# Order of loads, stores and norms in the head stage of a graph kernel

## The chip, the cores and the metric

The kernel runs on one core of one Trainium2 chip. The metric is the device time of one execution in microseconds (us); the median of several runs stands for a kernel. Besides, one execution is taken with the hardware profiler, and every view below is of that one.

## The reference

The input is x, 128 graphs of 128 nodes with 256 features, and an adjacency matrix for each graph. Layer 0 normalises x over the features, takes the positive part h, and computes from h a convolution branch (a 1x1 convolution, batch norm, relu, a convolution with 17 taps along the nodes, batch norm, relu with h added), a message branch and a gated recurrent cell. Layer 1 is a set of small graph convolutions on the first 25 nodes. All is in float32. The part that matters here is the beginning of layer 0:

```python
h = jnp.maximum(_layernorm(x, axis=-1), 0.0)
...
xc = jnp.transpose(x, (0, 2, 1))
h = _bn(_conv1d(xc, conv1_w, 0), bn1_g, bn1_b, bn1_m, bn1_v)
h = jax.nn.relu(h)
h = _bn(_conv1d(h, conv2_w, 8), bn2_g, bn2_b, bn2_m, bn2_v)
```

(the x inside the branch is the h of the first line).

## The kernel before, in words

The graphs are worked on in 32 blocks of four. The 17-tap convolution is done in the frequency domain: the nodes of a graph are transformed to 68 frequencies, multiplied there by the transformed taps, and transformed back. The kernel has three stages: the heads (from 0 to about 286 us), the spectral products (to about 466 us) and the gates with layer 1 (the rest).

The change lies in the heads. There the order of the instructions of every engine is the order in which the program writes them down (a manual schedule); each engine, and each queue that issues DMAs, works through its own list in that order and waits where an operand isn't ready. For each block the heads do the following.

- `head_load` (L198) brings the block's x to a tile `ln` of 0.5 MB. There are four such tiles (`ahead = 4`), so the load for block i+4 can start once the transposes of block i have read theirs. SP issues it.
- `head_stats` (L208, L209, L212 on DVE, L214 on GpSimd) gives mean and reciprocal deviation. It comes in two parts of two graphs each.
- `head_norm` (L221 and L227 on DVE, L224 on ACT) normalises: ACT does two graphs of the block, DVE the other two.
- `head_turn` transposes the block on PE (L237), ACT takes the positive part into a tile `ht` (L238), and SP stores it to DRAM (`htd`, L239) for the third stage. "Turn" in the text is this step.
- `head_conv1` multiplies by the 1x1 weights, in two halves (L251 on PE), and DVE's maximum with a row stands for batch norm's shift and relu (L254).
- `head_sums` makes even and odd parts on GpSimd (L262 to L264).
- `head_spectra` transforms the block before (L280 on PE; ACT L291 and DVE L289 copy to X).

Beside this run the spectra of the taps, 16 units in all. A unit has three steps, each a batch of small matmuls (L180) whose results ACT (L189) and in part DVE (L187) copy to a tile `sp` of 2.2 MB, of which there are two. After its last step the unit is stored to DRAM (`vd`, L191); the spectral stage reads it back as `v` (L344). `some_spectra`, called `between` in the loop, does one step. The loop calls it twice in odd iterations (in the middle and at the end) and once in even ones (at the end), so that a unit takes two iterations; when a unit is found finished at the end of an odd iteration, its store is issued, the taps of a later unit are loaded (L166), and the next unit's first step is done in the same call.

Iteration i of the loop in `heads` works on several blocks at once: it turns block i+1, does conv1 for block i, takes statistics of block i+3, normalises block i+2 and transforms block i-1. So even blocks are turned in odd iterations. Its order before the change is: load of block i+4; statistics part 0; conv1 half 0; (odd: tap step); sums; norms; conv1 half 1; statistics part 1; turn and store of h; sums; tap step; spectra.

The PSUM banks of this stage are given out in a fixed rotation of eight: conv1 takes one for each half, a turn two, a tap step four, the spectra four. A matmul therefore waits until the engine that empties the bank given out eight before has done so.

Of the kernel before, what the change touches and what calls it, by code (L numbers as in the profile page):

```python
# [17 lines left out]
BB = 4  # L18
# [57 lines left out]
def gnn_kernel(ctx: ExitStack, tc: tile.TileContext, io, out0: bass.AP, out1: bass.AP):  # L76
# [94 lines left out]
    def weight_spectra(pool, c, q, w2):  # L171

        sp = pool.tile([P, LW, WCH], F32, tag="sp", name="sp", bufs=2)
        n = WCH // 4
        for s0 in range(0, n, STEP):
            s1 = min(s0 + STEP, n)
            ps = [bank() for _ in range(4)]
            for j in range(s1 - s0):
                for r in range(4):
                    nc.tensor.matmul(ps[r][:, j * LW:(j + 1) * LW], w2[32 * r:32 * r + KW, s0 + j, :],  # L180
                                     gt[32 * r:32 * r + KW, :], start=True, stop=True)
            for r in range(4):
                o0 = r * n + s0
                dst = sp[:, :, o0:o0 + s1 - s0]
                s = ps[r][:, :(s1 - s0) * LW].rearrange("p (j d) -> p d j", d=LW)
                if r == 3 and s1 < n:
                    nc.vector.tensor_copy(dst, s)  # L187
                else:
                    nc.scalar.copy(dst, s)  # L189
            yield  # L190
        nc.sync.dma_start(vd[c, q], sp)  # L191


    xs, stats, hcs, h1s, evens = ({} for _ in range(5))
# [1 line left out]
    def head_load(pool, ahead, i, queue):  # L196
        xs[i] = pool.tile([P, BB, D], F32, tag="ln", name="ln", bufs=ahead)
        queue.dma_start(xs[i], x[i])  # L198
# [28 lines left out]
            nc.vector.tensor_scalar(xs[i][:, b, :], xs[i][:, b, :], mv[:, b, 0:1], rs[:, b:b + 1],  # L227
                                    op0=ALU.subtract, op1=ALU.mult)

    def head_turn(wk, i):  # L230

        ln = xs.pop(i)
        ht = wk.tile([P, C, T], F32, tag="ht", name="ht", bufs=2)
        for c in range(C):
            ps = bank()
            for b in range(BB):
                nc.tensor.transpose(ps[:, b * N:(b + 1) * N], ln[:, b, c * P:(c + 1) * P], ident)  # L237
            nc.scalar.activation(ht[:, c, :], ps, AF.Relu)  # L238
        nc.sync.dma_start(htd[i], ht)  # L239
        hcs[i] = ht  # L240

# [52 lines left out]
    def heads(wk, xk, ep, ahead, X, between, consts):  # L294

        for i in range(NBLK + 1):
            more = i < NBLK
            if i + ahead < NBLK:
                head_load(xk, ahead, i + ahead, nc.sync)
            if i == 0:  # L300
                head_conv1(wk, 0, 0)
                between()
                head_sums(ep, 0, 0)
                head_norm(1, wk)
                head_conv1(wk, 0, 1)
                head_turn(wk, 1)
                head_sums(ep, 0, 1)
                head_stats(wk, 2)
                between()
                head_norm(2, wk)  # L310
                head_stats(wk, 3)
                continue
            if i + 3 < NBLK:
                head_stats(wk, i + 3, (0,))
            if more:
                head_conv1(wk, i, 0)
            if i % 2:
                between()
            if more:
                head_sums(ep, i, 0)  # L320
            if i + 2 < NBLK:
                head_norm(i + 2, wk, BB // 2)
            if more:
                head_conv1(wk, i, 1)
            if i + 3 < NBLK:
                head_stats(wk, i + 3, (1,))
            if i + 1 < NBLK:
                head_turn(wk, i + 1)
            if more:
                head_sums(ep, i, 1)  # L330
            between()
            head_spectra(X, i - 1)
            if i == 2:
                next(consts)
# [72 lines left out]
    with front as es:  # L407
        hk = es.enter_context(tc.tile_pool(name="hk", bufs=1))
        xp = es.enter_context(tc.tile_pool(name="xp", bufs=1))
        X1 = xp.tile([P, C, NP_ - NB, 2, P], F32)  # L410
        order = es.enter_context(ExitStack())
        order.enter_context(tc.manual_schedule(engines={nc.gpsimd.engine}))
        early = es.enter_context(ExitStack())
        xe = early.enter_context(tc.tile_pool(name="xe", bufs=1, side="right"))
        X0 = xe.tile([P, C, NB, 2, P], F32)
        X = X0, X1
        with ExitStack() as ws:

            ws.enter_context(tc.manual_schedule())

            xk = ws.enter_context(tc.tile_pool(name="xk", bufs=1, side="right"))
            wp = ws.enter_context(tc.tile_pool(name="wp", bufs=1))
            ahead = 4
            todo = [(c, q) for c in range(C) for q in range(D // WCH)]
            nc.scalar.dma_start(gt, io["gt"])
            nc.scalar.dma_start(vec, io["vec"])

            taps = [taps_load(wp, *todo[0], nc.sync, split=4, amid=[lambda: head_load(xk, ahead, 0, nc.sync)])]
            spectra = []
            ones = X1[:, 0, 0].rearrange("p k g -> p (k g)")  # L430
            nc.vector.memset(ones, 1.0)

            def rouse(n):
                ps = bank()
                for _ in range(n):
                    nc.tensor.matmul(ps[:, :2 * P], ones[:, :P], ones, start=True, stop=True)

            def some_spectra(k=1):
                for _ in range(k):
                    if not spectra and todo:  # L440
                        spectra.append(weight_spectra(wp, *todo.pop(0), taps.pop(0)))
                    if spectra and next(spectra[0], STOP) is STOP:
                        spectra.pop(0)
                        if len(todo) > 1:
                            taps.append(taps_load(wp, *todo[1], nc.sync))
                        some_spectra()

            constant_loads()
            head_load(xk, ahead, 1, nc.sync)
            taps.append(taps_load(wp, *todo[1], nc.sync))  # L450
            for k in range(2, ahead):
                head_load(xk, ahead, k, nc.sync)
            nc.sync.dma_start(fw, row("fw", 5))
            consts = constants(wp)
            head_stats(hk, 0)
            rouse(3)
            some_spectra()
            rouse(4)
            next(consts)
            some_spectra()  # L460
            next(consts)
            head_norm(0)
            next(consts)
            rouse(2)
            head_turn(hk, 0)
            head_stats(hk, 1)
            some_spectra()
            heads(hk, xk, wp, ahead, X, some_spectra, consts)
            while spectra or todo:
                some_spectra()  # L470
        turns.close()
        banks[:] = [ctx.enter_context(tc.tile_pool(name="psum", bufs=8, space=bass.MemoryType.PSUM, reuse_waits="tile")), None]

        bp = es.enter_context(tc.tile_pool(name="bp", bufs=1, reuse_waits="tile"))
        spectral(bp, (X0, 0), 0, NB, {})
        early.close()
        gw = ctx.enter_context(tc.tile_pool(name="gw", bufs=1, side="right", reuse_waits="tile"))
        idm = gw.tile([P, N], F32)
        wms = gw.tile([P, C, 2, MW], F32)
        bms = gw.tile([P, 2, MW], F32)  # L480
        swm = gw.tile([P, 3, MW], F32)
        wih = gw.tile([P, 2 * C, 3 * D], F32)
        whh = gw.tile([P, C, 3 * D], F32)
        sw = [gw.tile([P, 3, 3, P], F32, name=f"sw{k}") for k in range(3)]

        def gate_load(to, what):
            tc.keep_in_program_order(nc.sync.dma_start(to, what))

        def gate_loads():
            gate_load(wms, io["wms"].rearrange("(c p) (q o) -> p c q o", p=P, q=2))  # L490
            yield
            gate_load(idm, io["idm"])
            gate_load(bms.rearrange("p q o -> p (q o)"), row("bms", 2 * MW))
            for name, w in (("whh", whh), ("wih", wih)):
                for c in range(w.shape[1]):
                    yield
                    gate_load(w[:, c], io[name][c * P:(c + 1) * P])

        loads, sums = gate_loads(), gate_weights()

        def gate_steps(p):
            next(loads, None)
            if p in (36, 40, 44, 52, 56, 60, 64):
                next(sums, None)

        amid = {p: lambda p=p: gate_steps(p) for p in range(NB, NP_, 4)}
        spectral(bp, (X1, NB), NB, NP_, amid)
        for _ in sums:
            pass
        order.close()  # L510
# [799 lines left out]
```

## Time and profile before

| | us |
|---|---|
| runs, median of 3 | 1870.97 |
| runs, lowest to highest | 1866.61 to 1873.89 |
| the profiled execution | 1868.6 |
| its span, first to last instruction | 1866.8 |
| PE busy in the span | 1824.8 (98%) |
| DVE busy | 1359.8 (73%) |
| GpSimd busy | 790.4 (42%) |
| ACT busy | 732.3 (39%) |

A busy PE isn't PE at its peak, since matmuls are pipelined and their ends are modelled. What decides is the chain of work that ended last: it follows the last instruction back, at each step to what released it. Over the whole span 82% of it is PE, 9% DMA (7% loads of x) and 4% DVE. In windows of 20 us the heads show PE at 16.6 to 20 us busy, DVE at 12 to 18, ACT at 9 to 16, DMA at shares of 0.66 to 0.87, and a granted PE clock between 0.83 and 1.0 of full speed; the spectral stage after 300 us shows PE at 20 of 20 and the clock at 1.0.

In the views, PE is the matmuls and PEld their weight loads, POOL is GpSimd, SPq is SP's queue of DMA issues, and L251 is line 251 of the kernel. "<-" names what ended a wait.

### The profile page before, as it was taken

Reading aid. Unit: us, or ns where it says so; the run is one execution under the profiler, and the core shown is the slowest. Engines: PE = TensorE matmul, PEld = TensorE weight load, DVE = VectorE, ACT = ScalarE, POOL = GpSimd, SP = SyncE. Lnnn points to the kernel's source line nnn. Section 1 sums busy time; section 2 is a strip of 40 time slices with the busy share of each in tenths; the row PEclk is TensorE's granted clock in tenths of the full one; section 3 lists DMA queues with packets and bytes.
Section 4 is the critical chain, followed back from the end, with each engine's and each line's share of the span. In section 5 each row is a group of like instructions: output and inputs, shape, how many; then the busy total and the mean of one; then the engine's idle time right before and its main releaser. Section 6 shows DMA issues by size and latency. Waiting matters only on the chain.

```text
span 1866.8 us, 34711 instructions
## 1 busy us (share of the span) xinstructions
PE 1824.8 (98%) x12552; PEld 1581.5 (85%) x12552; DVE 1359.8 (73%) x3331; ACT 732.3 (39%) x1624; POOL 790.4 (42%) x993
## 2 busy tenths in 40 slices
PE   8898999999999999999999999999999999999998
PEld 6777787888888888888788888888788888888787
DVE  6776766777887888788656678887756678787553
ACT  5555551111434333343344443343343443333334
POOL 4665665577344354354312235444412243544100
PEclk9899999999999999999999999999999999999999
DMA  7777769998733333334324433334333433332134
GB/s 286 274 282 282 277 272 305 337 334 268 229 90 77 86 83 84 76 85 113 83 82 109 128 94 75 74 79 117 73 82 94 120 106 86 82 72 79 24 95 135
DMA packets 279870, 267.47 MB, mean 143 GB/s; under 512 B 170870, under 2 KB 247371, under 8 KB 277651
## 3 DMA queue, kind: packets, MB, share of 16 engines
q1 hardware_dynamic: 274515, 247.32, 45.8%
q10 hardware_dynamic: 5184, 17.93, 2.4%
q8 instruction: 100, 1.64, 0.4%
q14 instruction: 71, 0.58, 0.1%
HBM read 168.84 MB, written 96.35 MB: 142 GB/s over the span
## 4 chain that ended last, share of the span: by engine, by line
PE 82%; DMA 9%; DVE 4%; POOL 1%; SPq 1%; issue 1%; ACT 0%; DVEq 0%; ACTq 0%; POOLq 0%
PE bank L714 43%; DMA ln<-in_x_dram 7%; PE bank L371 6%; PE bank L1041 5%; PE bank L982 5%; PE bank L615 5%; PE bank L366 3%; PE bank L665 3%; PE bank L594 3%; PE bank L251 3%; PE bank L280 1%; PE bank L961 1%; PE bank L891 1%; DMA nt<-in_adjN_dram 1%; PE bank L571 1%
## 5 line engine op out<-in xcount | busy, mean ns | idle before, releaser
L714 PE MATMUL bank<-t,sw 128*128 128x256 f32 x1152 | 291.9, 380 | 0.8 <-POOL t L689 0.4
L727 POOL TENSOR_TENSOR u<-u,m 128x256 f32<-128x256 f32 x128 | 94.9, 741 | 463.8 <-ACT m L725 409.0
L714 PEld LDWEIGHTS bank<-t,sw 128*128 128x128 f32 x1152 | 215.0, 191 | 33.4 <-issue 2.8
L714 PE MATMUL bank<-t,wih 128*128 128x256 f32 x768 | 200.3, 384 | 0.0
L714 PEld LDWEIGHTS bank<-t,wih 128*128 128x128 f32 x768 | 143.5, 190 | 29.0 <-DVE o L754 6.6
L251 PE MATMUL bank<-wc,ht 128*128 128x256 f32 x512 | 134.9, 416 | 0.0
L363 POOL TENSOR_TENSOR vs<-v 128x256 f32<-128x256 f32 x134 | 101.0, 779 | 57.0 <-DMA v<-vd 30.5
L251 PEld LDWEIGHTS bank<-wc,ht 128*128 128x128 f32 x512 | 101.8, 207 | 18.7
L714 PE MATMUL bank<-xc,wih 128*128 128x256 f32 x384 | 114.9, 381 | 0.9 <-ACT xc L598 0.8
L714 PE MATMUL bank<-t,whh 128*128 128x256 f32 x384 | 114.7, 380 | 0.1
L714 PE MATMUL bank<-xn,wih 128*128 128x256 f32 x384 | 114.3, 379 | 0.0
L1041 PE MATMUL bank<-w,hh 128*125 128x256 f32 (+9 forms) x480 | 113.6, 380 | 0.1
L714 PE MATMUL bank<-ht,whh 128*128 128x256 f32 x384 | 110.3, 381 | 0.3 <-DVE m L625 0.3
L638 ACT ACTIVATE msg<-msg 128x512 f32<-128x512 f32 x64 | 36.8, 622 | 182.0 <-DVE msg L634 182.0
L598 ACT ACTIVATE xc<-xc,bn 128x512 f32<-128x512 f32 x64 | 46.2, 722 | 150.4 <-DVE xc L597 150.4
L1041 PEld LDWEIGHTS bank<-w,hh 128*125 128x125 f32 (+9 forms) x480 | 84.6, 178 | 18.0 <-DVE hh L987 1.2
L982 PE MATMUL bank<-ax,w 128*128 128x500 f32 (+9 forms) x352 | 94.5, 404 | 1.0 <-DVE xc L597 1.0
L732 DVE TENSOR_TENSOR u<-bank,u 128x256 f32<-128x256 f32 x128 | 53.5, 418 | 50.2 <-PE bank L714 49.6
L208 DVE BATCH_NORM_STATS2 st<-ln 128x6 f32<-128x256 f32 x128 | 51.8, 405 | 51.1 <-DMA ln<-in_x_dram 51.1
L368 ACT COPY k<-bank 128x256 f32<-128x256 f32 x67 | 25.0, 372 | 145.8 <-PE bank L366 68.7
L714 PEld LDWEIGHTS bank<-xn,wih 128*128 128x128 f32 x384 | 73.1, 190 | 9.8
L714 PEld LDWEIGHTS bank<-xc,wih 128*128 128x128 f32 x384 | 72.2, 191 | 10.5 <-ACT xc L598 1.4
(224 smaller groups left out, 4582.5 us busy)
## 6 DMA issues: line engine op xcount, KB each, us to landing
vd<-sp SPq DMA_DIRECT2D x16, 2176.0 KB
v<-vd SPq DMA_DIRECT2D x34, 1024.0 KB
w<-in_w_dram SPq DMA_DIRECT2D x40, 512.0 KB
ln<-in_x_dram SPq DMA_DIRECT2D x32, 512.0 KB
htd<-ht SPq DMA_DIRECT2D x32, 512.0 KB
yd<-ys ACTq DMA_DIRECT2D x32, 512.0 KB
ht<-htd SPq DMA_DIRECT2D x64, 256.0 KB
ym<-yd SPq DMA_DIRECT2D x32, 512.0 KB
```

The source lines that it names most:

```text
L251: nc.tensor.matmul(pv[:, s, :], ht[:, c, (2 * h + s) * N:(2 * h + s + 1) * N], wc1[:, c, :], start=c == 0, stop=c == C - 1)
L363: nc.gpsimd.tensor_tensor(vs[:, c], vi[c], vr[c], op=ALU.subtract)
L366: nc.tensor.matmul(p1[:, :D], a[:, c], vs[:, c], start=c == 0, stop=c == C - 1)
L371: nc.tensor.matmul(ps[:, k * D:(k + 1) * D], u[:, c], w[c], start=c == 0, stop=c == C - 1)
L594: nc.tensor.matmul(ps[:, b * N:(b + 1) * N], ym[:, 2 * h + b, o * P:(o + 1) * P], idm, start=False, stop=b == 1)
L615: nc.tensor.matmul(ps[:, b, :], d[:, b * N:(b + 1) * N], w, start=True, stop=True)
L665: nc.tensor.matmul(ps[:, b * N:(b + 1) * N], msg[:, b, c * P:(c + 1) * P], e[:, b, :], start=True, stop=True)
L714: nc.tensor.matmul(ps, w, d, start=n == 0, stop=n == len(pairs) - 1)
L727: nc.gpsimd.tensor_tensor(got["u4"], got["u2"], got["m5"], op=ALU.add)
L732: nc.vector.tensor_tensor(got["u3"], ps, got["u2"], op=ALU.add)
L982: nc.tensor.matmul(pv[:, q - q0, :], w1s[k5 + g][:, c, q * P:(q + 1) * P], xv[:, c], start=c == 0, stop=c == C - 1)
L1041: nc.tensor.matmul(ps[:n1, :D], hh[:, q, at:at + n1], w2s[k5 + g][:, q, :], start=q == 0, stop=q == HID // P - 1)
```

## The change

Four things are altered, all in the heads.

1. The load of x for block i+5 is issued in iteration i, inside the turn, between ACT's relu and the store of h. Before, the load of that block was issued at the start of iteration i+1. (The first turn, before the loop, issues the load of block 4.)
2. In iterations from 1 on, the norms of block i+2 come first, ahead of conv1's first half and its maximum; the first part of the statistics of block i+3 comes after the sums, where the norms were.
3. A finished unit of tap spectra isn't stored at once. Two halves of it, each 68 of the 136 columns, are put on a list, and each later tap step first issues one half from that list.
4. The loop after the heads runs until that list is empty, too.

```diff
-        nc.sync.dma_start(vd[c, q], sp)
+        for d in range(0, LW, LW // 2):
+            stores.append((vd[c, q, :, d:d + LW // 2], sp[:, d:d + LW // 2]))
...
-    def head_turn(wk, i):
+    def head_turn(wk, i, reload=None):
...
             nc.scalar.activation(ht[:, c, :], ps, AF.Relu)
+        if reload:
+            reload()
         nc.sync.dma_start(htd[i], ht)
...
-            if i + ahead < NBLK:
-                head_load(xk, ahead, i + ahead, nc.sync)
+            reload = None
+            if i + 1 + ahead < NBLK:
+                reload = lambda i=i: head_load(xk, ahead, i + 1 + ahead, nc.sync)
...
-            if i + 3 < NBLK:
-                head_stats(wk, i + 3, (0,))
+            if i + 2 < NBLK:
+                head_norm(i + 2, wk, BB // 2)
             if more:
                 head_conv1(wk, i, 0)
             if i % 2:
                 between()
             if more:
                 head_sums(ep, i, 0)
-            if i + 2 < NBLK:
-                head_norm(i + 2, wk, BB // 2)
+            if i + 3 < NBLK:
+                head_stats(wk, i + 3, (0,))
...
             if i + 1 < NBLK:
-                head_turn(wk, i + 1)
+                head_turn(wk, i + 1, reload)
...
+            def some_spectra():
+                if stores:
+                    nc.sync.dma_start(*stores.pop(0))
+                advance()
...
-            head_turn(hk, 0)
+            head_turn(hk, 0, lambda: head_load(xk, ahead, ahead, nc.sync))
...
-            while spectra or todo:
+            while spectra or todo or stores:
                 some_spectra()
```

`advance` is the old body of `some_spectra`.

## The prediction

> **What bounds the kernel now.** Read first: the chain of work that ended last, in order of time, for the first 300 us. From about 33 to 240 us it consists of two kinds of link, PE's matmuls and loads of x (the columns are start, length, what ended last):
>
> ```profile
> 155.28 11.92 DMA ln<-in_x_dram
> ...
> 172.92 12.06 DMA ln<-in_x_dram
> ...
> 190.67 11.45 DMA ln<-in_x_dram
> ...
> 207.82 12.12 DMA ln<-in_x_dram
> ...
> 273.02 7.98 DMA vd<-sp
> 281.07 9.40 DMA v<-vd
> ```
>
> A load of x takes some 12 us from issue to use, once every two blocks (17.7 us). So the heads are bound by loads in every second iteration, and by PE between them. The second view, the sums of waits up to 500 us, says who waits (us in total, times, longest):
>
> ```profile
> DVE st L208 <- DMA ln<-in_x_dram: 51.1, 14, 5.5
> PE bank L180 <- DVE h L254: 18.4, 9, 3.6
> SPq L239 <- ACT ht L238: 208.1, 32, 11.2
> ```
>
> DVE's statistics wait 51.1 us for x. They stand in DVE's order ahead of conv1's maximum, which frees PE's bank; so PE's tap matmuls wait for L254. The third line is harmless by itself, but it shows SP sitting on each store of h until ACT has made h: whatever follows on SP's queue goes out after that. Why a load takes 12 us is seen in the timeline of one block's end:
>
> ```profile
> 188.95 0.33 SPq L239 DMA_DIRECT2D htd<-ht  x1
> 189.37 0.38 SPq L191 DMA_DIRECT2D vd<-sp  x1
> 189.85 0.73 SPq L166 DMA_DIRECT2D w<-in_w2t_dram  x1
> 190.67 1.15 SPq L198 DMA_DIRECT2D ln<-in_x_dram  x1
> ...
> 202.14 0.43 DVE L208 BATCH_NORM_STATS2 st<-ln 128x6 f32<-128x256 f32 x1 [4.18 <-DMA ln<-in_x_dram]
> ```
>
> 0.5 MB of h, 2.2 MB of spectra and 0.5 MB of taps are queued ahead of x. Last, windows (PE, PEld, DVE, ACT, POOL busy; granted clock, DMA share, GB/s):
>
> ```profile
> 203.50:206.50 3.00, 2.06 (x80) 1.79 (x84) 2.95 (x8) 2.49 (x6) 2.31 (x3) 1.00 0.02 7
> 207.00:210.00 3.00, 3.00 (x7) 2.40 (x8) 2.23 (x9) 0.96 (x5) 2.87 (x4) 0.50 1.07 440
> 249.09:256.50 7.41, 7.41 (x130) 6.17 (x129) 5.11 (x17) 4.89 (x14) 4.58 (x7) 1.00 0.75 290
> 256.50:263.05 6.55, 6.55 (x113) 5.73 (x112) 6.38 (x22) 3.97 (x12) 5.53 (x8) 1.00 0.62 254
> ```
>
> The DMA engines idle while everybody waits; afterwards the clock is halved and the matmuls take longer; the last two lines are a pair of blocks that lost nothing.
>
> **What the Trainium skill says.** "DMA: Bandwidth & Descriptors", "Queues, rings and completion order": what one engine issues goes into one row of rings, consumed in ring order. The trace agrees: x lands after all that SP issued before it. The same page, "Anatomy of one DMA", gives a DMA some 2 us beyond its bytes, mostly the receipt of the last write. For the last store of spectra the trace has 7.98 us for 2.2 MB behind one store of h; I use that. "TensorE: Matmul & The Clock Gate", Part 1: idle time lowers the clock, 3.4 us of activity raises it again; the trace shows 0.50 at 207 to 210.
>
> **What is lost now.** The transposes of a block ("turn", L237) begin at 249.09 (block 27), 256.50 (28), 263.05 (29): undisturbed, an odd block's turn is followed after 7.41 us by the even one, and this after 6.55 by the next odd one. Even to odd, the L237 starts of blocks 2 to 28 give 7.35, 12.01, 7.67, 14.10, 6.84, 12.27, 6.54, 12.67, 7.50, 10.03, 10.95, 10.01, 11.91, 6.55: together 136.4 against 14 x 6.55 = 91.7. So 44.7 us are lost, waits and halved clock together. The odd-to-even intervals (7.41 to 7.82) lose next to nothing.
>
> **Part 1, the load of x ahead of h's store, with norms ahead of the maxima.** The load for block j leaves right after the transposes of block j-4 instead of at the next iteration's start, and the statistics follow the first half of conv1 and its sums. Slack grows from about 8 us to more than 9 even behind a store of spectra, and latency falls: at an odd block's turn nothing large is ahead (about 1.1 us wait for the transposes, 0.7 to the first packet, 1.5 for 0.5 MB at the 400 GB/s seen, 2 to land: 5.5 us). So the 44.7 us go, with the halved clock. DVE does the same work in another order: two norms (1.14 to 1.70) stand where two statistics with aggregates (1.16) stood; conv1's maximum comes up to 0.5 later, and its bank is wanted only 0.97 us into the turn. I take 0. If DVE (11.5 of 13.97 busy) had no room it would be 0.4 an iteration, 12 us; a gain here I exclude since PE is full. h's store is delayed by one load, 1.5 us; it is read hundreds of us later, and its buffer two turns later: 0.
>
> **Part 2, spectra in two halves a tap step later.** The same bytes, 16 more issues (0.38 each on SP, which idles: 0). In the built program's order on SP both halves stand directly behind h's store of the odd block's turn, where before they stood behind that of the even one, a whole iteration (6.5 to 7.4 us) earlier. Neither half waits for an engine, so both leave at once. What is new is a wait: two sp buffers, so ACT's and DVE's first copies (L189, L187) into a buffer, after the next even turn, need both halves landed. Formerly they had over 14 us, now 7.41 and a bit. Timed from the odd turn's start, by the turn at 249.09: h's store was issued at 250.88, +1.79; the halves follow at +2.2; 7.98 to land as measured at 273.02; and the load of x now ahead holds h's store, which would start about +2.5, until +3.3: 0.8 more. They land at +11.0. Needed: PE's next conv1 begins 2.98 after a turn (252.07 - 249.09) in the bank of ACT's first tap copy, 0.54 long (1.61 / 3): the copy must start by 7.41 + 2.98 - 0.54 = +9.85. So PE loses 11.0 - 9.85 = 1.15 us, 14 times: 16.1 us. Behind ACT's waiting copy are two more, the copies of X and the norms; behind DVE's the copies of X, the norms, conv1's maximum. DVE is done with the norms about 6.4 after the even turn, the next turn is then at 7.7: they aren't later than PE. Bounds: 0 if load and store overlap and land at +9.8; 2.4 if the store is as slow as those before (1.3 more, a load running into it).
>
> **Part 3, the end.** The last store goes out behind h's store of block 31 (turn 276.44) instead of 30 (270.81): 5.6 us later against PE's end of the heads. The first v loads are queued behind it (281.07 follows the landing), PE already waits for them (1.97 at 287.63), nothing covers it: +5.6. PE then idles some 7 us instead of 2, so the clock stays low longer: between 0 and 1.7, I take 0.4. Together 6.0 (0 to 7.3; 0 if v's loads needn't wait).
>
> **Sum.** The profiled execution takes 1868.6 (span 1866.8 and 1.8 around it): 1868.6 - 44.7 + 16.1 + 6.0 = 1846.0. The runs' median, 1870.97, stands 2.4 above it: 1848.
>
> **Rivals.**
> A: The halves land in time (a store overlaps the load ahead). Stall 0: 1868.6 - 44.7 + 6 + 2.4 = 1832. For it: DMA share 0.62 to 0.75 in the undisturbed pair. Against: 7.98 us is measured with little beside it.
> B: The store's wait takes most of the load's place: 2.2 us each, 30.8: 1863. For it: loads of x and taps run into the store's end as today.
> C, slower: the wait for sp outgrows the old one. It decides from (44.7 - 6.0) / 14 = 2.8 us, landing at +12.6; at 3.5 us with the clock halved again (0.6 each) it is 57 us: 1868.6 - 44.7 + 57 + 6 + 2.4 = 1889. For it: PE idled 2 to 3.6 us before each halving. Against: the store would have to take 10 us instead of 8.
> D: The loads don't come earlier where it counts: SP still issues them behind a wait for PE's transposes; then 1869 to 1877. Against: the order on SP shows load, h, halves.
>
> **Chances.** Forecast 0.56 (its own range 1840 to 1858), A 0.16, B 0.17, C 0.06, D 0.05. A change of under 0.5% (9.4 us) can't be told from none: faster is below 1861.6, which holds forecast and A and half of B, 0.81; same, the rest of B and most of D, 0.13; slower 0.06. The range reaches from A, 1830, to 1864 with most of B.
>
> **What would show it.** Right: no wait of the statistics for x; even-to-odd intervals of 7 to 8.5; ACT's or DVE's L189/L187 waiting for vd; stores landing about 11 us after the odd turn; v's first matmul later against the last turn (by some 6 us). Wrong: L189 never waits (A), waits over 2 us (B, C), or halved clocks remain.

## The result and the profile after

The changed kernel takes 1893.4 us (median of 4 runs, 1889.9 to 1895.5) against 1869.4 before: a ratio of 1.0124 with a 95% interval of 1.0097 to 1.0151. It is slower by 24 us, outside the range, and on the side of rival C. The profiled execution took 1889.9 with a span of 1888.1 (before: 1866.8).

The sums of waits in the first 320 us say at once what has taken the place of the old wait (us in total, times, longest):

```profile
ACT sp L189 <- DMA vd<-sp: 49.4, 14, 4.7
DVE sp L187 <- DMA vd<-sp: 43.2, 14, 4.4
...
PE bank L254 <- ACT sp L189: 40.0, 14, 4.0
...
DVE st L209 <- DMA ln<-in_x_dram: 4.1, 1, 4.1
```

The statistics wait for x once instead of 14 times. But ACT's first copy into an sp buffer waits for the store of that buffer's previous unit, all 14 times that there is one, and PE waits 40.0 us for that copy. In the chain of work that ended last, the links that were loads of x are now stores of spectra:

```profile
184.48 1.09 ACT ht L239 x2
...
186.44 9.90 DMA vd<-sp
...
196.44 0.51 ACT sp L189
...
196.99 1.47 PE bank L254 x3
...
202.87 1.09 ACT ht L239 x2
...
204.83 9.66 DMA vd<-sp
```

One such pair of blocks in the timeline of all engines: block 19 is turned at 183.79, SP issues both halves directly after h's store, block 20 is turned at 191.21, and ACT's copy is late.

```profile
184.86 0.33 SPq L199 DMA_DIRECT2D ln<-in_x_dram  x1
185.59 0.33 SPq L242 DMA_DIRECT2D htd<-ht  x1
185.97 1.78 SPq L453 DMA_DIRECT2D vd<-sp  x2
...
191.21 1.04 PE L238 MATMUL bank<-ident,ln 128*128 128x128 f32 x8
...
192.27 0.33 SPq L199 DMA_DIRECT2D ln<-in_x_dram  x1
...
196.44 1.31 ACT L189 COPY sp<-bank 128x408 f32<-128x408 f32 x3 [3.46 <-DMA vd<-sp]
...
196.99 5.35 PE L254 MATMUL bank<-wc,ht 128*128 128x256 f32 x16 [2.73 <-ACT sp L189]
```

The halves were issued at 185.97, 2.2 us after the turn, and landed at 196.34 (the second, issued at 186.44, took 9.90): 12.6 after the turn. PE idled 2.73 us. And the 16 matmuls of conv1 then took 5.35 us instead of 3.72. The windows show why (PE, PEld, DVE, ACT, POOL busy; granted clock, DMA share, GB/s): right after that wait the clock was halved, after the wait before 215.14 it wasn't.

```profile
197.50:200.50 3.00, 3.00 (x9) 2.36 (x8) 1.09 (x5) 1.92 (x7) 0.00 (x0) 0.53 0.51 205
...
215.14:218.70 3.56, 3.56 (x17) 3.10 (x17) 3.09 (x12) 2.42 (x8) 0.72 (x1) 1.00 0.60 239
```

Where the span's 21.3 us come from, by the starts of the turns: the 14 intervals from an even to the next odd block add up to 154.3 us (before 136.4), +17.9; the 13 from odd to even are 7.41 each, -2.1; the beginning and the last blocks, -1.9. So the last turn starts at 290.35 instead of 276.44, +13.9. From there to the first product of the spectral stage it is 15.2 us instead of 11.2, +4.0. Right after it 1.75 are lost: the 17th product of the stage comes 7.62 us after the first instead of 5.88, and from there on the two stages run alike. The last 1.6 fall in the rest of the kernel, whose program is the same. This is the first product, after and, at 287.63, before:

```profile
305.56 1.19 PE L358 MATMUL bank<-v,X 128*128 128x256 f32 x2 [5.99 <-DMA v<-vd]
...
308.98 2.90 PE L358 MATMUL bank<-v,X 128*128 128x256 f32 x6 [0.52 <-DMA v<-vd]
```

```profile
287.63 0.67 PE L354 MATMUL bank<-v,X 128*128 128x256 f32 x2 [1.97 <-DMA v<-vd]
```

### The profile page after: what moved, and what is told of

It reads as the page before. It is cut to its first block, busy times and chain, and to the rows that moved or that the text cites. A ratio compares the mean times of both kernels' runs of the same rounds, so it can differ in the third digit from the quotient of the medians.

```text
span 1888.1 us, 34691 instructions
## 1 busy us (share of the span) xinstructions
PE 1825.6 (97%) x12552; PEld 1580.3 (84%) x12552; DVE 1355.7 (72%) x3331; ACT 732.1 (39%) x1624; POOL 787.9 (42%) x993
## 4 chain that ended last, share of the span: by engine, by line
PE 82%; DMA 9%; issue 3%; ACT 2%; DVE 2%; SPq 1%; POOL 1%; ACTq 0%; DVEq 0%; POOLq 0%
PE bank L722 44%; DMA vd<-sp 8%; PE bank L375 6%; PE bank L1049 5%; PE bank L623 5%; PE bank L990 5%; PE bank L370 3%; PE bank L673 3%; PE bank L602 3%; PE bank L254 2%; PE bank L969 1%; PE bank L899 1%; DMA nt<-in_adjN_dram 1%; PE bank L579 1%; ACT ht L239 1%
## 5 line engine op out<-in xcount | busy, mean ns | idle before, releaser
L254 PE MATMUL bank<-wc,ht 128*128 128x256 f32 x512 | 142.9, 434 | 40.0 <-ACT sp L189 40.0
L254 PEld LDWEIGHTS bank<-wc,ht 128*128 128x128 f32 x512 | 107.2, 217 | 62.0 <-ACT sp L189 42.0
L189 ACT COPY sp<-bank 128x408 f32<-128x408 f32 (+1 forms) x160 | 66.8, 505 | 63.6 <-DMA vd<-sp 49.4
L363 DVE TENSOR_TENSOR s<-X 128x256 f32<-128x256 f32 x67 | 45.7, 683 | 49.5 <-PE bank L375 49.3
```

The lines of the kernel that those rows point to most:

```text
L254: nc.tensor.matmul(pv[:, s, :], ht[:, c, (2 * h + s) * N:(2 * h + s + 1) * N], wc1[:, c, :], start=c == 0, stop=c == C - 1)
```

## The experiments

The theory after the result: the loads and the norms did what they should; storing the unit a tap step later puts its landing behind the next use of its sp buffer, and the wait halves PE's clock besides. The rivals: the early loads crowd the DMA rings, so that stores land late wherever they are put; or the halves are slow as such. Ratios are to the kernel before, run on the same chip beside each group.

| kernel | median us | ratio (95% interval) |
|---|---|---|
| change, unit stored whole and at once | 1830.7 | 0.9786 (0.9754 to 0.9819) |
| before, late halves alone | 1913.9 | 1.0233 (1.0203 to 1.0263) |
| change, both halves at once | 1831.1 | 0.9789 (0.9760 to 0.9819) |
| before, loads early alone | 1832.5 | 0.9795 (0.9770 to 0.9819) |
| change, one half at once, one late | 1841.0 | 0.9837 (0.9819 to 0.9855) |
| change, last unit at once | 1892.6 | 1.0117 (1.0096 to 1.0137) |
| change, whole at once, taps loaded ahead (the fast kernel) | 1827.7 | 0.9767 (0.9752 to 0.9783) |
| change, PE's idle time filled | 1878.4 | 1.0039 (1.0026 to 1.0052) |
| the fast kernel again | 1827.5 | 0.9769 (0.9749 to 0.9790) |
| the fast kernel, last unit late | 1831.2 | 0.9789 (0.9770 to 0.9808) |
| before, norms first alone | 1836.6 | 0.9823 (0.9800 to 0.9845) |

A third sp buffer, which should take the wait away by itself, was not tried.

### The late store, undone and alone

The change with the unit stored whole and at once:

```diff
-        for d in range(0, LW, LW // 2):
-            stores.append((vd[c, q, :, d:d + LW // 2], sp[:, d:d + LW // 2]))
+        nc.sync.dma_start(vd[c, q], sp)
```

> The changed kernel with one part undone: a finished unit of spectra is stored whole and at once, as before; loads and norms stay as changed. Theory (the late store makes the next user of its sp buffer wait, and the end of the heads is pushed back): no wait of L189 or L187 for vd, none of the statistics for x, even-to-odd intervals near 6.6, the first product of the spectral stage some 9 to 14 us earlier against the last turn than in the changed kernel; 1825 to 1838 us. Rival (loads of x sent ahead of h's store crowd the DMA rings, so that stores land late wherever they are put): L189 still waits, 1870 to 1890.

Measured: 1830.7. No wait for vd is left in the heads, and the even-to-odd intervals are 7.0 us in the mean. The first product came at 249.0, 10.8 us after the last turn (238.20): 4.4 us earlier than in the changed kernel, not the 9 to 14 that were expected. The late halves on the kernel before, with loads and norms untouched:

```diff
-        nc.sync.dma_start(vd[c, q], sp)
+        for d in range(0, LW, LW // 2):
+            stores.append((vd[c, q, :, d:d + LW // 2], sp[:, d:d + LW // 2]))
...
+                if stores:
+                    nc.sync.dma_start(*stores.pop(0))
```

> The kernel before with one part of the change alone: the spectra stored in two halves, a tap step later; loads and norms stay as before. Theory: the store goes out behind the h of the odd block's turn, so L189 waits for vd after each even turn, and the loads of x queued behind it are still late; both waits fall into the same interval, so together 1880 to 1900. Rival (the early loads are to blame): 1865 to 1872, no wait of L189.

Measured: 1913.9, above the upper end. The waits of this kernel:

```profile
ACT sp L189 <- DMA vd<-sp: 52.6, 12, 5.6
PE bank L252 <- ACT sp L189: 52.6, 14, 4.9
```

The theory's place is right, with one thing that it hadn't foreseen. In SP's order the load of x at the start of the next iteration now lies between the two halves, so the second half lands later still (13.7 us after the odd turn in the mean, instead of 12.8 in the changed kernel; PE waits 52.6 us instead of 40.0), and the statistics have no wait of their own left: they wait behind the same copies. The two runs together rule the rival out as the cause of the wait: without early loads the wait is there, with early loads and an early store it isn't. Its mechanism is there all the same. With the early loads a unit stored at once lands 13.0 us after the turn that it stands behind (mean of the 11 units behind the turns of blocks 6 to 26); with norms first and store at once but without early loads (below) the same units, issued just as soon after the turn, land after 11.5. Stored at once, a unit has the time; stored late, it doesn't.

### The halving

```diff
         for d in range(0, LW, LW // 2):
-            stores.append((vd[c, q, :, d:d + LW // 2], sp[:, d:d + LW // 2]))
+            nc.sync.dma_start(vd[c, q, :, d:d + LW // 2], sp[:, d:d + LW // 2])
```

> The changed kernel with the delay alone undone: both halves are issued in the step that finds the unit finished, one after the other. Theory (the delay costs, the halving doesn't): within 3 us of the whole store at once, 1825 to 1840. Rival (two stores of 1.1 MB are slower than one of 2.2[...]): 10 us or more above the whole store at once.

Measured: 1831.1, as the whole store at once. Two stores of 1.1 MB cost nothing that can be seen here, and they don't land later either: the 11 units behind the turns of blocks 6 to 26 land 12.9 us after the turn in halves and 13.0 whole.

### How late is too late

The first half at once, the second a tap step later:

```diff
-        for d in range(0, LW, LW // 2):
-            stores.append((vd[c, q, :, d:d + LW // 2], sp[:, d:d + LW // 2]))
+        nc.sync.dma_start(vd[c, q, :, :LW // 2], sp[:, :LW // 2])
+        stores.append((vd[c, q, :, LW // 2:], sp[:, LW // 2:]))
```

> The changed kernel with the first half of a unit stored at once and only the second half a tap step later. Theory (the wait comes from when the last byte of the unit lands, not from storing late as such): in the changed kernel 2.2 MB behind the odd turn land 12.7 us after it, 2.8 us too late; 1.1 MB less at some 0.31 us per 0.1 MB brings that to about 9.3, just before the 9.85 that PE needs: L189 waits under 5 us in all, no halved clock, and only the end of the heads is late by some 3 us; 1832 to 1842. Rival (any store behind the odd turn's loads is late, since the loads crowd it): half the wait stays, 1860 to 1880.

Measured: 1841.0, within the range. With half the bytes behind the odd turn the wait shrinks from 40.0 us to 8.6, where under 5 were expected:

```profile
PE bank L254 <- ACT sp L189: 8.6, 10, 2.0
```

The second halves land 10.4 us after the odd turn in the mean, not the 9.3 expected, and one halved clock is left, after a wait of 1.97 us. So the landing of the last byte decides, and half the bytes are still somewhat late.

### What the halved clock costs

Work is added here: 14 matmuls of the identity, into unused columns of a bank, for each unit from the third on, where PE is about to wait.

```diff
+            if s0 == 0 and (c or q > 1):
+                for _ in range(14):
+                    nc.tensor.matmul(ps[0][:, STEP * LW:STEP * LW + 96], ident, ident[:, :96], start=True, stop=True)
```

> The changed kernel with work added: 14 matmuls of the identity into unused columns of a bank, once for each unit from the third on, where PE is about to wait for the spectra's store. Theory (each wait of some 2.9 us also halves PE's clock, which makes the following conv1 take 5.3 instead of 3.7 us): the added matmuls fit into the wait, the clock stays, and the kernel gets faster by up to 14 x 1.6 = 22 us: 1868 to 1882. Rival (the clock doesn't matter, conv1 is slow because its operands come late): 1893 or more, by what the matmuls overrun.

Measured: 1878.4, faster by 15 us than the changed kernel with less work. The chain of one pair and its window:

```profile
189.04 0.91 PE bank L180 x24
189.95 3.29 PE bank L184 x28
193.24 1.11 PE bank L286 x64
194.35 3.65 PE bank L257 x16
```

```profile
188.00:197.84 9.84, 9.84 (x142) 8.90 (x140) 5.49 (x18) 4.06 (x11) 4.47 (x6) 1.00 0.83 319
```

The added matmuls (L184, 28 machine instructions) take 3.29 us, conv1 (L257) is back at 3.65, and the clock stays at 1.00. The interval is 9.84, the undisturbed 6.55 and the 3.29; the copies are hardly waited for any more (0.8 us in all). The 14 intervals add up to 142.8, so 51.1 us are lost there, 46.1 of them the filling (14 x 3.29), where the changed kernel loses 62.6, though PE's waits in it are only 40.0: the filling is longer than the wait that it covers and still cheaper than the wait and the slow matmuls after it.

### The end of the heads

The change, but the last of the 16 units stored at once:

```diff
+        if c == C - 1 and q == D // WCH - 1:
+            nc.sync.dma_start(vd[c, q], sp)
+            return
```

> The changed kernel with the last of the 16 units alone stored whole and at once. Theory (the late last store holds back the first product of the spectral stage by 4 us, with a clock that starts halved): 4 to 7 us less than the changed kernel, 1886 to 1890, and the first product about 11 us after the last turn instead of 15. Rival (the spectral stage makes up for a late start, or its loads wait for other things): within 2 us of the changed kernel.

Measured: 1892.6, no difference that can be told, as the rival has it; yet in the trace the first product comes 11.0 us after the last turn (305.1 and 294.06), as the theory has it. The heads before it happened to be 3.7 us longer in this execution, although their program is the same up to there. This run settles nothing: the halved clocks make the heads vary by as much as is looked for. So the reverse was tried where no such noise is, on the fast kernel (below): its last unit alone stored late.

```diff
+        last = c == C - 1 and q == D // WCH - 1
+        n = LW // 2 if last else LW
+        for d in range(0, LW, n):
+            stores.append((vd[c, q, :, d:d + n], sp[:, d:d + n]))
...
+                    if todo:
+                        nc.sync.dma_start(*stores.pop(0))
...
+                if stores and not (spectra or todo):
+                    nc.sync.dma_start(*stores.pop(0))
```

> The fast kernel (loads early, norms first, taps loaded ahead of a whole store at once) with the last of the 16 units alone stored late, in two halves a tap step later as in the change. No sp buffer is taken again after it, so that only the end of the heads can change. Theory (a late last store delays the first product of the spectral stage by some 4 us, with the clock halved longer): 3.5 to 6.5 us above the fast kernel run beside it. Rival (the spectral stage makes up for it): within 1.5 us.

> The fast kernel once more, as what the late last unit is compared with on the same chip: 1825 to 1830.

Measured: 1831.2 against 1827.5 on the same chip, +3.7 at the lower end of what was expected (the runs, 1829.8 to 1832.1 and 1824.5 to 1829.9, just overlap). The first product comes 15.2 us after the last turn (247.1 and 231.87) instead of 10.3 (243.5 and 233.19).

### Loads alone, norms alone

The kernel before with the load of x in the turn, nothing else:

```diff
+        if reload:
+            reload()
         nc.sync.dma_start(htd[i], ht)
...
-            if i + ahead < NBLK:
-                head_load(xk, ahead, i + ahead, nc.sync)
```

> The kernel before with one part of the change alone: the load of x in the turn, ahead of h's store; norms stay behind conv1's first maximum, the spectra are stored whole and at once. Theory (earlier loads give the 44.7 us back, the place of the norms gives little): 1825 to 1845, at most 10 us above the kernel that has the norms first too. Rival (without the later statistics the loads still come too late in every second iteration): 1850 to 1869, statistics waiting for x over 20 us.

Measured: 1832.5, as the theory expected: 38.4 us less than before. With the norms first too it is 1830.7, and the difference of 1.8 is within the intervals. The kernel before with norms first, nothing else:

```diff
-            if i + 3 < NBLK:
-                head_stats(wk, i + 3, (0,))
+            if i + 2 < NBLK:
+                head_norm(i + 2, wk, BB // 2)
             if more:
                 head_conv1(wk, i, 0)
```

> The kernel before with one part of the change alone: norms ahead of conv1's first maximum, statistics part 0 after the sums; loads and stores as before. Theory (statistics then wait for x about 4 us later in the iteration and no longer hold conv1's first maximum, so that part of the 44.7 us goes even without earlier loads): 1840 to 1862. Rival (the wait only moves to the second maximum): 1865 to 1874.

Measured: 1836.6, below the range. The loads are no earlier, and statistics still wait for them:

```profile
DVE st L208 <- DMA ln<-in_x_dram: 25.6, 10, 4.1
...
PE bank L180 <- DVE h L254: 0.8, 1, 0.8
```

25.6 us of DVE's waiting remain, but of PE's waiting behind conv1's maximum little does: 0.8 us ahead of L180 (18.4 before) and 7.5 ahead of L280 (4.6 before). Either edit alone gives nearly the whole gain, so they don't add up.

### A version that beats both

With the store whole and at once, two odd-to-even intervals stood out in the trace, 9.02 and 8.77 us instead of 7.41. The load of the taps was put ahead of the store, which stays in the step that finds the unit finished:

```diff
-        nc.sync.dma_start(vd[c, q], sp)
+        stores.append((vd[c, q], sp))
...
                         taps.append(taps_load(wp, *todo[1], nc.sync))
+                    nc.sync.dma_start(*stores.pop(0))
                     advance()
```

> Loads early and norms first as changed, the unit stored whole in the step that finds it finished, but the load of a later unit's taps issued ahead of that store instead of behind it. Theory (with loads of x early PE is the bound, and the few odd-to-even intervals of 8.8 to 9.0 us instead of 7.4 are PE's tap matmuls waiting for taps queued behind a store): these intervals fall to 7.4, and the time by 2 to 6 us against the whole store at once, 1825 to 1829. Rival (those intervals come from elsewhere): the same within 2 us, 1829 to 1833.

Measured: 1827.7, and 1827.5 when run again, 2.3% below the kernel before. The gain of 3 us over the whole store at once is within what the intervals leave open; in the trace one interval of 8.5 us remains (150.19 to 158.67), and one of 8.2 in the trace of the second run. That the taps caused the long intervals is not shown.

## Why the prediction was wrong

**What bounds the kernel** was right: loads of x in every second iteration, at the price named. Taking them away (loads early, norms first, store at once) gave 40.1 us against the 44.7 predicted.

**Part 1** was right in size, wrong in its credit: it took early loads and late statistics as one remedy. Each nearly suffices. Its cost for DVE, taken as 0, was 0: with both edits most intervals are 6.54 and 7.41. (The four terms of the latency of x add up to 5.3, not 5.5; nothing rests on it. Its 2 us to land come from a section headed for DMAs that GpSimd issues, while SP issues these; measured, the loads at the odd turns of blocks 3 to 27 land 3.8 to 5.2 us after their issue, where 0.7, 1.5 and 2 make 4.2.)

**Part 2 failed**, in its landing time and in the clock. It named the right wait, on the right lines, 14 times, and the right deadline; by its working PE loses 1.15 us each time, 16.1 in all. The intervals lost 154.3 - 91.7 = 62.6. Two terms of the sum were wrong.

First, the load of x ahead of the store. The landing was put at 2.2 to the issue, 7.98 for the store and 0.8 for the load ahead: 11.0 us after the odd turn. It was 12.8 in the mean of the 14 units that are waited for (11.4 to 13.8; 12.6 in the pair shown). The issue and the store were right, the load was not, as two units at the end of the heads show:

```profile
260.05 0.33 SPq L199 DMA_DIRECT2D ln<-in_x_dram  x1
...
261.15 1.61 SPq L453 DMA_DIRECT2D vd<-sp  x2
268.19 11.23 SPq L242 DMA_DIRECT2D htd<-ht  x2
279.51 1.85 SPq L453 DMA_DIRECT2D vd<-sp  x2
```

```profile
261.63 9.86 DMA vd<-sp
```

The unit stored at 279.51 has no load of x ahead of it and none behind it. By the landing times that the trace records it lands 10.3 us after its turn, as 2.2 + 7.98 has it. The unit stored at 261.15 has a load ahead and none behind it, and lands 12.5 after its turn. So the load ahead costs some 2.2 us, not 0.8; the same two units differ by 1.9 with the last unit at once and by 2.5 with the idle time filled. The load at the next turn, which the prediction kept as a bound of 1.3 more, isn't needed for the wait. Why 0.5 MB ahead cost that much is open. By an estimate from these numbers, late halves with no load of x ahead of them or between them would cost PE 10.3 - 9.85 = 0.5 us a time; that wasn't tried. PE's wait is 40.0 / 14 = 2.86 instead of 1.15, 23.9 us more.

Second, the clock, put at nothing in the heads. The forecast has no halved clock, since it expected waits of 1.15 us; only rival C has it. Of the 62.6, 22.6 are not PE's wait for the copy. After ten of the 14 waits the 16 matmuls of conv1 took 5.3 to 6.6 us instead of 3.72, together 19.5 more. Filling the wait with work took 15 us off the kernel, though this work was longer than the wait.

**Part 3** named the right wait: 6.0 predicted, 4.0 to the first product and 1.75 behind it in the profile of the change; on the fast kernel 3.7 in the medians.

**The rivals.** C was what happened: 1889 for it, 1893 measured. That the numbers are so close is partly luck, since C took a wait of 3.5 us and 0.6 for the clock, and the runs have 2.86 and some 1.6. It was given 0.06, because the store "would have to take 10 us instead of 8"; from the first half's issue to the landing of the second it took 10.5 in the mean. The 7.98 was measured at the emptiest place of the trace before. Thirteen other stores there (31.70 to 242.37), with x queued behind them, took 8.4 to 9.7, and none of these had a load of x just ahead, as the change puts it. C's argument "PE idled 2 to 3.6 us before each halving" isn't quite what the trace before has: a wait of 1.60 us (before 239.82) was followed by a halved clock, one of 2.62 (before 186.82) was not.

**The range** ended at 1864, short of its own upper working (a wait of 2.4 each and 7.3 at the end give 1867), and without the clock, which adds to every wait.

## What to carry to other kernels

A store that is moved later isn't free because nobody reads its result soon: the buffer that it empties is wanted again, so count from its new issue to its landing and compare that with the next writer. Take the landing time from a store that has the same traffic before and behind it; the time of a quiet one is right only for a quiet place. When several edits cure one wait, price each alone, since one may be enough and another may be all cost.

## What the runs showed of the hardware

The cost of a wait on PE isn't the wait alone. The Trainium skill, "TensorE: Matmul & The Clock Gate", Part 1, lets the clock fall after an idle window of about 3.4 us. In the trace of the changed kernel waits of 2.73 and 2.69 us (before 196.99 and 272.14) and one of 1.71 (before 32.99) were followed by conv1 at 5.3 to 5.4 us, while waits of 2.50, 2.96 and 3.28 (before 215.14, 143.93 and 161.23) left it at 3.72. So waits much shorter than the window can do it, and their length alone doesn't decide.

Where the wait falls does much of it. All changes of the granted clock in this trace lie on one grid of 3.41 us. These are three steps of the grid around the wait of 3.28 and two around that of 2.73 (columns as in the windows of the result):

```profile
155.96:159.38 3.42, 1.99 (x88) 1.72 (x88) 1.01 (x5) 0.71 (x2) 2.08 (x3) 1.00 1.01 353
159.38:162.79 3.41, 1.56 (x7) 1.41 (x8) 2.09 (x8) 2.11 (x8) 1.03 (x2) 1.00 0.87 346
162.79:166.20 3.41, 3.41 (x31) 2.93 (x33) 2.87 (x10) 1.59 (x4) 2.09 (x3) 1.00 0.10 38
...
193.51:196.92 3.41, 0.75 (x52) 0.60 (x42) 0.46 (x1) 0.48 (x2) 3.11 (x4) 1.00 0.96 363
196.92:200.34 3.42, 3.35 (x8) 2.72 (x9) 1.67 (x8) 2.50 (x9) 0.00 (x0) 0.50 0.61 244
```

The longer wait is split over two steps, with PE idle for 1.43 and 1.85 us, and the clock stays; the shorter one lies in one step, with PE idle for 2.66, and the next step has half the clock. In this trace's heads every step at full clock with more than 2.0 us of idle PE was followed by one at half; of those with 1.7 to 1.9 some were and some weren't. Matmuls of no use, put into the wait, kept the clock up and made the kernel 15 us faster.
